# Where attention scores are accumulated: two PSUM banks or six, for the first twenty-one score chunks

## The chip, the core and the metric

The kernel runs on one core of a Trainium2 chip. The core has five engines, each with its own in-order queue of instructions: TensorE (PE in the profile; its weight loads are listed apart, as PEld), VectorE (DVE), ScalarE (ACT), GpSimd (POOL) and SyncE (SP, which here only issues DMAs). They wait for one another by semaphores. Matmuls write into PSUM, which this kernel divides into eight banks of 128 partitions by 512 fp32 values; results leave PSUM through ScalarE and VectorE.

The metric is the device time of one execution in microseconds (us). Before the change the median of three runs is 2384.47 us (2383.08 to 2388.02).

## What is computed

One transformer block on x of shape (2, 2048, 1024), fp32: a pre-norm single-head attention with head size D = 256, then a pre-norm feed-forward part.

```python
x = x + attn(layernorm(x))
x = x + ffn(layernorm(x))

def attn(x):                      # B=2, S=2048, D=256
    q, k, v = split(x @ Wqkv + bqkv)
    p = softmax(q @ k.T / sqrt(D))        # 2048 x 2048 for each of the two sequences
    return (p @ v) @ Wo + bo

def ffn(h):
    rw = sum(top2(h @ gate_w))
    shared = relu(h @ up_w) ** 2 @ down_w
    routed = ((h @ fc1_w @ expert_w) * rw) @ fc2_w
    return layernorm(shared + routed, ln_gamma, ln_beta)
```

## The kernel before

**Precision.** Every large product is made of three fp32r matmuls (`Pass3`, line 117): an operand is split into a high and a low part (`split`, line 140: a cast on ScalarE, a subtraction on VectorE), and high·high, low·high and high·low are added up in one PSUM bank. All these matmuls have line 130 in the profile, so they are told apart by the tile they write.

**Stages.** The 4096 tokens form eight query blocks of 512. First come normalisation and the projections to q, k and v for each block (tiles `pv`, `pq`), in an order written out by hand (`manual_schedule`). Then comes attention (lines 701 to 761), one query block after the other, and then the feed-forward part (from line 1007, again ordered by hand), which takes the rest of the time.

**Attention for query block n.** The 2048 keys of a sequence form 16 chunks of 128.

- `scores(n, k)` (line 545) makes chunk k: two contractions of 128, three matmuls each, so six matmuls of 512 columns into one bank `ps`. ScalarE copies the bank to SBUF (line 557), and VectorE takes the running elementwise maximum from the same bank (line 562; for chunk 0 a second ScalarE copy, line 560).
- `row_max(n)` (line 564), after chunk 15: four small transposes (`pmx`), a reduction on VectorE (line 571), four more transposes (`pmb`).
- `softmax(n, j)` (line 578), for chunks 2j and 2j+1 together: subtract the maximum (line 586, VectorE), exponential (line 587, ScalarE), then a split into the high part (line 142, ScalarE) and the low part (line 143, VectorE) of `p`, and a running sum (lines 593 and 595, VectorE).
- `values(n, k)` (line 597): six matmuls for each chunk, into two banks `po` that stay open over all 16 chunks.
- `finish(n)` and `project(n)` (lines 608 and 629): the row sums (`psum`), the output projection (`pw`, 48 matmuls) and the residual, whose rows come in by DMA from SP and get the bias added by a DMA from POOL.

**Which block runs with which.** `scores(0, 0..15)` stand alone: they come right after the last projection (line 667), with no other large product beside them. Then `start(1)` splits the q of block 1, and `row_max(0)` follows. From there the loop at line 709 pairs `scores(n, k)` with `values(n-1, k-lag)`. For n = 1 the lag is `LAG + 2` = 5, so `scores(1, 0..4)` also come with no `values` beside them. For n > 1 the lag is 3.

**PSUM pools.** `psa` has four banks, `psb` two, `psc` two. Before the change every `ps` bank is one of the two of `psb`. `psa` serves `pv` and `pq` before attention, and `po` (two banks for a whole block) and `pw` within it. `psc` serves the small transposes and the row sums. A bank is handed to its next user when the last reader of the former one is done.

**What sets the order.** The projections and the feed-forward part have their order written out. For attention the Tile framework lays out each engine's queue when the program is built: among instructions that are ready by its own estimate of durations, the one that comes first in the program goes first. On the chip each queue then runs in that fixed order. The POOL queue also carries, within attention, copies and sums of weight matrices for the feed-forward part in DRAM (`sum_step`, line 387).

Of the kernel before, what the change touches and what calls it, by code (L numbers as in the profile page):

```python
# [25 lines left out]
def kernel(  # L26
# [47 lines left out]
    psa = ctx.enter_context(tc.tile_pool(name="psa", bufs=4, space=PSUM))  # L74
    psb = ctx.enter_context(tc.tile_pool(name="psb", bufs=2, space=PSUM))
# [5 lines left out]
    def unit(name, dtype=FR):  # L81
        return up.tile([P, U], dtype, tag="u", name=name)
# [7 lines left out]
    def half(name):  # L90
        return hp.tile([P, W], FP, tag="h", name=name)

    def bank(pool, name):
        return pool.tile([P, W], FP, tag="b", name=name)
# [309 lines left out]
    def hl(t):  # L404

        return t.rearrange("p (s n) -> p s n", s=2)
# [122 lines left out]
    def load_kv(name, src, alloc):  # L529
        t = alloc(name)  # L530
        nc.sync.dma_start(out=f32(t), in_=src)
        return t

    st = {}

    def kv_home(j):
        return ex_unit if j < 2 * BPB - 1 else unit

    def kv_chunk(n, i, k):
        return kv[(n // BPB) * BPB + k // 4][i]  # L540
# [4 lines left out]
    def scores(n, k):  # L545
        s = st[n]
        if k % 4 == 0:
            s["s"].append(unit(f"s{n}_{k // 4}", FP))
        pm = bank(psb, "ps")
        acc = Pass3(pm, NDC)  # L550
        kk, q = hl(kv_chunk(n, 0, k)), hl(s["q"])
        for dc in range(NDC):
            acc.add(
                tuple(kk[:, i, ds(dc * W + (k % 4) * P, P)] for i in range(2)),
                tuple(q[:, i, ts(dc, W)] for i in range(2)),
            )
        nc.scalar.copy(s["s"][k // 4][:, ts(k % 4, W)], pm)  # L557
        if k == 0:
            s["max"] = half(f"max{n}")
            nc.scalar.copy(s["max"], pm)  # L560
        else:
            nc.vector.tensor_tensor(s["max"], pm, s["max"], ALU.max)  # L562
# [34 lines left out]
    def values(n, k):  # L597
        s = st[n]
        if k == 0:
            s["o"] = [Pass3(bank(psa, "po"), NKC) for _ in range(NDC)]  # L600
        v = hl(kv_chunk(n, 1, k))
        for dc in range(NDC):
            s["o"][dc].add(
                tuple(v[:, i, ds((k % 4) * D + dc * P, P)] for i in range(2)),
                tuple(hl(s["p"][k // 2])[:, i, ts(k % 2, W)] for i in range(2)),
            )
# [47 lines left out]
    def a_block(i, norm, xT, x3):  # L654
# [5 lines left out]
        def after(j):  # L660
            if i + 1 == NBLK:
                if j == 0:
                    x3()
                elif j == 2 * NB - 1:
                    start(0, load_row(q_d[0]))
                    for k in range(NKC):
                        scores(0, k)
                    start(1, load_row(q_d[1]))
                    row_max(0)
                return  # L670
            if j == 0:
                x3()
            if j < NB:
                norm.step(j)
            if j == NB - 1:
                norm.step(NB)
                if i + 2 < NBLK:
                    after_next.append(NormBlock(load_block(xf, order[i + 2], nc.gpsimd)))
                nxt.append(new_xT(f"a{i}"))
            elif j > NB:  # L680
                split_tile(norm.x[j - NB - 1], j - NB - 1, nxt[0])
# [22 lines left out]

    g_f = half("g_f")[:, : NCC * NE].rearrange("p (c e) -> p c e", c=NCC)
    nc.gpsimd.dma_start(out=g_f, in_=gate_w.rearrange("(c p) e -> p c e", p=P))
    LAG = 3
    xts = []
    for n in range(1, NBLK + 1):
        if n == NBLK:  # L710
            X = {p: (unit("xh"), unit("xl")) for p in ("p1", "p2")}

        lag = LAG if n > 1 else LAG + 2
        for k in range(NKC + lag):
# [5 lines left out]
            if n < NBLK and k < NKC:  # L720
                scores(n, k)
            if k >= lag:
                values(n - 1, k - lag)
                if n == BPB and (k - LAG) % 4 == 3:
                    j = BPB + (k - LAG) // 4
                    kv[j].append(load_kv(f"v{j}", v_d[j], kv_home(j)))
# [281 lines left out]
    with tc.manual_schedule():  # L1008
        for b in range(NBB):
# [70 lines left out]
            for m, (p, i) in enumerate(UP):  # L1080
# [4 lines left out]
                ps = acc[i].ps  # L1085
# [52 lines left out]
                elif m >= 2 * NK and p != "p7":  # L1138
                    n = {"p4": "p6", "p6": "p5", "p5": "p3", "p3": "p7"}[p]
# [31 lines left out]
            def y_at(r, c, t):  # L1171
                return y[2 * r + t // 2][:, ds((t % 2) * C + c * W, W)]
# [9 lines left out]
            for j, p in enumerate(("p1", "p2", "p6", "p5", "p3", "p7", "p4")):  # L1182
# [12 lines left out]
                for k in range(NK - late):  # L1195
# [4 lines left out]
                    if more:  # L1200
# [3 lines left out]
                        if j >= 5 and k % 2 and k < 2 * NB:  # L1204
                            n = "p1" if j == 5 else "p2"
# [22 lines left out]
                for t in range(NB):  # L1228
                    for s, w in last if late else ():
                        down(t, s, w)  # L1230
                    ps, u, v = accs[t].ps, y_at(1, 0, t), y_at(1, 1, t)
# [72 lines left out]
```

## Time and profile before

| | us |
|---|---|
| median of three runs | 2384.47 |
| profiled execution | 2384.76 |
| its span (first to last instruction) | 2382.9 |
| outside the span | 1.9 |
| PE busy | 2335.8 (98%) |
| PEld busy | 1921.8 (81%) |
| DVE busy | 1461.4 (61%) |
| ACT busy | 1131.4 (47%) |
| POOL busy | 298.1 (13%) |
| first to last start of a `ps` matmul | 309.2 to 719.1 |

A matmul of 512 columns is shown with a duration of about 390 ns, but consecutive ones overlap: they start about 227 ns apart when nothing is in the way. So a PE that is shown busy can still lose time in small pieces, and time lost is better found from the starts than from the busy share. A row of a timeline gives start, duration, engine, line, what is written from what, and in brackets the idle time of the engine before it with the instruction that ended it. A row of the chain gives start, duration and what held it.

### The profile page before, as it was taken

What the parts mean: (1) busy time and instruction counts of PE and PEld (TensorE: products, weight loads), DVE (VectorE), ACT (ScalarE), POOL (GpSimd) and SP (SyncE); (2) the same over time, 40 slices, a digit from 0 to 9 for tenths busy, and PEclk for the clock granted to TensorE, in tenths of its full rate; (3) what the DMA queues carried; (4) which work ended last, traced back from release to release, by engine and by line L of the source; (5) the groups of instructions that cost most, each with busy time, mean ns of one, the idle gap of its engine ahead of it and who ended that gap; (6) DMA issues with size and microseconds to landing.
All of it is one profiled execution on the core that took longest, in us unless ns stands there. A gap on an engine that the chain in (4) does not pass through costs nothing.

```text
span 2382.9 us, 29281 instructions
## 1 busy us (share of the span) xinstructions
PE 2335.8 (98%) x10704; PEld 1921.8 (81%) x10704; DVE 1461.4 (61%) x2168; ACT 1131.4 (47%) x1846; POOL 298.1 (13%) x450
## 2 busy tenths in 40 slices
PE   8999999999998999999999999999999999999998
PEld 7888878888886778788778888878888877888886
DVE  5566459888877466697746467644446563445545
ACT  6555455555444543676552374644145454214224
POOL 3222111012110010011210011210000010000001
PEclk9999999999999999999999999999999999999999
DMA  5977884999996666787997789997557798655695
GB/s 196 318 257 269 278 204 127 298 315 319 290 239 181 219 228 185 228 271 259 336 309 241 237 283 333 319 342 241 193 194 262 264 330 283 208 192 184 202 312 191
DMA packets 225807, 603.99 MB, mean 253 GB/s; under 512 B 18768, under 2 KB 80720, under 8 KB 223616
## 3 DMA queue, kind: packets, MB, share of 16 engines
q1 hardware_dynamic: 152160, 334.02, 41.2%
q0 software_dynamic: 73504, 268.11, 36.8%
q8 instruction: 85, 1.39, 0.2%
q14 instruction: 58, 0.48, 0.1%
HBM read 448.96 MB, written 210.76 MB: 277 GB/s over the span
## 4 chain that ended last, share of the span: by engine, by line
PE 88%; issue 5%; DMA 4%; DVE 1%; ACT 1%; POOL 1%; SPq 0%; POOLq 0%; DVEq 0%; ACTq 0%
PE pu L130 29%; PE pd L130 26%; PE ps L130 7%; PE pq L130 7%; PE po L130 7%; PE pv L130 4%; PE pw L130 3%; DMA w<-wt 1%; PE pg L872 1%; PE pf L130 1%; DMA xt<-xt_d 1%; DMA w<-w_p 1%; PE psum L619 1%; DMA res<-in_L_ffn_ln_beta_dram 0%; DMA ew<-in_L_ffn_expert_w_dram 0%
## 5 line engine op out<-in xcount | busy, mean ns | idle before, releaser
L130 PE MATMUL pd<-w,sp 128*128 128x512 f32 x3336 | 762.5, 390 | 11.0 <-DVE sp L1057 5.6
L130 PEld LDWEIGHTS pd<-w,sp 128*128 128x128 f32 x3336 | 626.5, 188 | 145.8 <-DVE sp L1057 8.4
L130 PE MATMUL pu<-xh,w 128*128 128x512 f32 x2240 | 694.4, 391 | 7.2 <-ACT w L815 5.1
L130 PEld LDWEIGHTS pu<-xh,w 128*128 128x128 f32 x2240 | 419.6, 188 | 99.0 <-ACT w L815 6.1
L130 PE MATMUL pu<-xl,w 128*128 128x512 f32 x1120 | 436.2, 389 | 0.0
L130 PEld LDWEIGHTS pu<-xl,w 128*128 128x128 f32 x1120 | 210.4, 188 | 44.1 <-DVE xl L150 0.4
L1052 ACT CAST sp<-h 128x512 fp32r<-128x512 f32 x238 | 145.9, 618 | 193.1 <-PE pd L130 160.7
L1057 DVE TENSOR_TENSOR sp<-h,sp 128x512 fp32r<-128x512 f32 x238 | 162.4, 687 | 100.9 <-ACT sp L1052 100.6
L815 ACT CAST w<-w 128x512 fp32r<-128x512 f32 x210 | 128.3, 617 | 178.4 <-DMA w<-wt 144.7
L130 PE MATMUL po<-p,v 128*128 128x512 f32 x768 | 197.0, 395 | 2.6 <-ACT p L142 2.4
L823 DVE TENSOR_TENSOR w<-w 128x512 fp32r<-128x512 f32 x210 | 143.1, 686 | 91.3 <-ACT w L815 84.8
L130 PE MATMUL ps<-q,k 128*128 128x512 f32 x768 | 195.9, 393 | 1.8 <-DVE max L562 1.8
L130 PEld LDWEIGHTS ps<-q,k 128*128 128x128 f32 x768 | 142.4, 188 | 36.1 <-DVE max L562 6.8
L130 PEld LDWEIGHTS po<-p,v 128*128 128x128 f32 x768 | 144.1, 190 | 33.6 <-ACT p L142 3.2
L1002 ACT ACTIVATE h<-h 128x1024 f32<-128x1024 f32 x48 | 50.7, 1055 | 208.7 <-DVE h L1110 159.7
L826 POOL DMA_DIRECT2D w_p<-w x140 | 75.1, 537 | 583.1 <-DVE w L823 532.3
L150 DVE TENSOR_TENSOR xl<-xt,xh 128x512 fp32r<-128x512 f32 x104 | 71.6, 688 | 122.8 <-ACT xh L149 120.8
L557 ACT COPY s<-ps 128x512 f32<-128x512 f32 x128 | 74.8, 585 | 148.2 <-PE ps L130 147.7
L213 DVE STREAM_TRANSPOSE xblk<-xrow 128x1024 f32<-128x1024 f32 x60 | 121.1, 2019 | 9.6 <-ACT xrow L283 9.6
L562 DVE TENSOR_TENSOR max<-ps,max 128x512 f32<-128x512 f32 x120 | 82.3, 685 | 44.4 <-ACT s L557 44.1
L130 PE MATMUL pq<-xha,w_h 128*128 128x512 f32 x256 | 99.7, 389 | 0.0
L130 PE MATMUL pq<-xha,w_l 128*128 128x512 f32 x256 | 99.7, 389 | 0.0
(181 smaller groups left out, 3034.3 us busy)
## 6 DMA issues: line engine op xcount, KB each, us to landing
w<-w_p SPq DMA_DIRECT2D x350, 512.0 KB, 4.2
w_p<-w POOLq DMA_DIRECT2D x140, 512.0 KB, 4.8
w<-wt SPq DMA_DIRECT2D x210, 256.0 KB, 3.7
xt_d<-xblk POOLq DMA_DIRECT2D x56, 512.0 KB, 4.6
xt<-xt_d POOLq DMA_DIRECT2D x56, 512.0 KB, 6.6
wt<-in_L_ffn_up_w_dram POOLq DMA_DIRECT2D x9, 2048.0 KB, 25.1
wt<-in_L_ffn_down_w_dram POOLq DMA_DIRECT2D x9, 2048.0 KB, 32.3
xres<-in_L_attn_x_dram SPq DMA_DIRECT2D x32, 512.0 KB, 13.0
```

Source lines behind the costliest of these rows:

```text
L130: nc.tensor.matmul(self.ps, lhsT=a, rhs=b, start=self.i == 0, stop=self.i == self.n - 1, skip_group_check=self.on,)
L150: late_ops.append(lambda: nc.vector.tensor_tensor(lo, t, f32(hi), ALU.subtract))
L213: nc.vector.transpose(b.rearrange("p (q k i) -> p q k i", q=P // SQ, i=SQ), r.rearrange("p (k i q) -> p q k i", k=NCC, i=SQ),)
L557: nc.scalar.copy(s["s"][k // 4][:, ts(k % 4, W)], pm)
L562: nc.vector.tensor_tensor(s["max"], pm, s["max"], ALU.max)
L619: nc.tensor.matmul(pt[:, t : t + 1], lhsT=s["sum"][:, ds(i * W + t * P, P)], rhs=ones, start=i == 0, stop=i == 1,)
L815: nc.scalar.copy(w[:, 0:W], f32(w)[:, W : 2 * W])
L823: nc.vector.tensor_tensor(w[:, W : 2 * W], v[:, W : 2 * W], v[:, 0:W], ALU.subtract)
L826: nc.gpsimd.dma_start(out=kept[key], in_=w.bitcast(FP))
L1002: nc.scalar.activation(o, v, AF.Relu)
L1052: nc.scalar.copy(t[:, 0:W], v)
L1057: add(t[:, W : 2 * W], v, f32(t)[:, 0:W], ALU.subtract)
```

## The change

`scores` takes its bank from `psb` or `psa` in turn for the first twenty-one chunks: of all sixteen of block 0 and of chunks 0 to 4 of block 1, those whose k is a multiple of three still use `psb`, and the others use `psa`. All later chunks use `psb` as before. `LAG` moves up in the file so that `scores` can read it. No instruction is added, removed or resized.

```diff
     st = {}
+    LAG = 3
...
         s = st[n]
         if k % 4 == 0:
             s["s"].append(unit(f"s{n}_{k // 4}", FP))
-        pm = bank(psb, "ps")
+
+        wide = n == 0 or n == 1 and k < LAG + 2
+        pm = bank(psa if wide and k % 3 else psb, "ps")
         acc = Pass3(pm, NDC)
...
-    LAG = 3
     xts = []
```

## The prediction

> **What bounds the kernel.** The page first: PE is busy 98% of the span, and the chain that ended last is 88% PE. So time is gained only where PE itself stands still. The next question is whether it does so where the diff acts. The chain around the start of attention, in order of time:
>
> ```profile
> 287.62 21.79 PE pq L130 x96
> 309.40 21.07 PE ps L130 x84
> ...
> 330.53 1.11 issue
> 331.63 0.70 DVE max L562
> 332.33 0.04 issue
> 332.37 3.04 PE ps L130 x12
> ```
>
> The projections run 96 matmuls in 21.79 us, 0.227 us each, with nothing in between: that is PE's pace. The scores then take 21.07 us for 84, 0.251 each. The timeline of two chunks of block 0 shows why:
>
> ```profile
> 317.62 3.99 PE L130 MATMUL ps<-q,k 128*128 128x512 f32 x15
> 318.04 1.23 PEld L130 LDWEIGHTS ps<-q,k 128*128 128x128 f32 x6 [0.23 <-DVE max L562]
> ...
> 318.29 0.58 ACT L557 COPY s<-ps 128x512 f32<-128x512 f32 x1 [1.02 <-PE ps L130]
> 318.91 0.69 DVE L562 TENSOR_TENSOR max<-ps,max 128x512 f32<-128x512 f32 x1 [0.92 <-ACT s L557]
> 319.65 1.23 PEld L130 LDWEIGHTS ps<-q,k 128*128 128x128 f32 x6 [0.38 <-DVE max L562]
> 319.75 0.59 ACT L557 COPY s<-ps 128x512 f32<-128x512 f32 x1 [0.88 <-PE ps L130]
> ```
>
> The reader is to see that the weight load of each chunk waits for the maximum of the chunk two before it. A bank is emptied by copy and maximum one after the other, from 318.29 to 319.60: 1.3 us, with about 0.1 more on either side. While one bank is emptied, PE fills the other in 6 x 0.227 = 1.36 us. So the bank comes back late each time. The copies at 316.68, 319.75 and 322.81 (each of the same bank) lie 3.07 us apart, 1.53 a chunk: 0.17 us lost on each.
>
> **How much is lost there.** From the starts of matmuls in the timeline: the first score matmul is at 309.24, the first of block 1 at 333.87, the first `po` at 344.03.
>
> - Block 0: 333.87 - 309.24 = 24.63 us, of which 96 x 0.227 = 21.79 is work. Lost: 2.84. Some 14 chunks at 0.17 make 2.4; the rest is one hiccup at 332.37, where the maximum stood behind the split of q (1.23 us, line 143).
> - The five chunks of block 1: 344.03 - 333.87 = 10.16 us, of which 30 x 0.227 = 6.81 and the eight small transposes 0.78 (335.53 to 335.91, 336.94 to 337.34) are work. Lost: 2.57. The largest piece is here:
>
> ```profile
> 342.53 1.23 PEld L130 LDWEIGHTS ps<-q,k 128*128 128x128 f32 x6 [1.80 <-DVE max L562]
> 342.53 1.66 PE L130 MATMUL ps<-q,k 128*128 128x512 f32 x6 [1.36 <-DVE max L562]
> ```
>
> Together 5.41 us is all that more banks could return.
>
> **The Trainium skill, twice.** By "TensorE: Matmul & The Clock Gate", section "Wait — 56ns, not 53.3ns?", warm matmuls of 512 columns start 215.7 ns apart. The row has 227. With the page's figure 126 matmuls would be 1.4 us shorter and the loss 6.8; the unstalled row of this very operation decides, 5.4. And one sentence speaks against the change: the same page, section "HAM oscillation — how this bites in real kernels", says of a tuned kernel that "Adding PSUM double-buffering gave no further gain". By it the sum would be 0. Here two buffers are there already, and the rows show that emptying a bank (1.5 with its gaps) takes longer than filling one (1.36), so I take the row.
>
> **The change, part by part.** Instructions and DMAs stay the same in number and size. What moves:
>
> 1. *Banks of block 0.* With six banks a chunk waits for the maximum of the sixth before it, and five fillings (6.8 us) lie between; ScalarE needs 0.58 and VectorE 0.69 of each 1.36 us, so neither falls behind. `psa` is free: its last users are `pq`, and the last of those is read by line 445 until 310.9; the others have long been read. PE then ends block 0 at 309.24 + 21.79 = 331.03, -2.84. The split of q for block 1 follows the copy of chunk 12 now (328.93, then the cast at 329.41); it should follow it again, some 1.8 us earlier, and be done by 329.9, so block 1 isn't kept waiting.
> 2. *The maximum and what hangs on it.* The last maximum ends at 335.38 now. Then it ends at 331.2 + 0.59 + 0.69 = 332.5, -2.9. Behind it in turn are the transposes, the reduction and the first subtraction (337.62 now), so about 334.7; the load of the exponential's table (1.28), the exponential (1.06), a copy (0.5) and the cast (1.05) give the first high part of `p` at 339.7 (342.70 now).
> 3. *The five chunks of block 1.* PE ends them at 331.03 + 6.81 + 0.78 = 338.6. That is 1.1 us before `p` is there. If nothing stood in between, PE would wait and the gain would be 4.3. But chunk 5 comes ahead of the values in the program, its `psb` bank (chunk 0's) has been read by then, and it takes 1.36, so PE is covered: 5.4. I take the upper end, less 0.3, since the transposes at 335.53 waited 0.29 for the maximum and will again: 5.1.
> 4. *What is late next: VectorE.* In this stretch it is full:
>
> ```profile
> 344.00:382.00 38.00, 38.00 (x175) 31.41 (x173) 36.11 (x39) 23.72 (x32) 0.00 (x0) 1.00 0.21 37
> 382.00:439.00 57.00, 57.00 (x263) 47.14 (x263) 46.72 (x57) 30.06 (x39) 10.15 (x12) 1.00 0.87 233
> ```
>
> (Window, its length, then busy time of PE, PEld, DVE, ACT and POOL.) VectorE is ahead by 2.9, PE by 5.1. The last low part of `p` ends at 377.1 and the last `po` matmul of the block at 381.75; after that part only four matmuls (0.9) must follow, so the block could have ended at 378.0. That leaves 3.7 of slack, and 2.9 + 3.7 = 6.6 is more than 5.1. Inside the stretch a part may be late, but PE has ten score chunks to fill in with. Bounds: gain 2.9 if VectorE decides throughout, 5.4 if never.
> 5. *The rest.* From 344 to 733 PE is busy without a break (57.00 of 57.00 us in the second row, and so in the blocks after it), so a lead is kept. The inputs of the projections come early enough: the bias for the last rows of block 6 lands at 714.91 and they are used from 727.7, 12.8 us of slack. The POOL and SP queues keep their items; their transfers fill the DMA engines (share 1.04 from 400 to 700), but PE waits for none of them. The feed-forward part starts from the end of attention and moves with it.
>
> Sum: the span falls from 2382.9 to 2377.8. The profiled execution (2384.76) is 0.3 above the median, so the same 5.1 is taken from the median: 2384.47 - 5.1 = 2379.4, 0.21% less.
>
> **Rivals.**
>
> - *VectorE decides block 1.* For it: 36.11 of 38.00 busy, and high parts that PE took within tenths of a microsecond of their end. Against it: the slack of 3.7 at the end. Gain 2 to 3.5, about 2381.6.
> - *The banks aren't free when wanted,* `psa` being held by `pq` or kept for `po`, and the change does little: 0 to 1 us, 2384. Against it: the reads of `pq` end by 310.9, and `po` needs two of four.
> - *Another order, slower.* The queues of attention are laid out anew when the program is built, with other bank times. The weak place is where attention ends:
>
> ```profile
> 757.39 9.45 DMA w<-wt
> 766.86 0.62 ACT w L815
> 767.47 0.97 ACT s L587
> 768.46 1.24 DVE sum L595
> 769.70 0.04 issue
> 769.74 3.58 PE psum L619 x16
> ```
>
> A weight transfer of 9.45 us holds a cast on ScalarE, the last exponential stands behind that cast, and PE loses 5.3 and 2.8 us between 761 and 770. Its matmuls after that start 0.43 us apart for a while, 12 x 0.2 = 2.5 us more. If one more such cast or tile load lands ahead of an exponential, it costs about 8 + 2.5 = 10.5. Against the gain: 2384.5 - 5.1 + 10.5 = 2389.9. It decides from a cost of about 10 us on. For it: nothing fixes that order. Against it: the blocks from 2 to 6 repeat 57.3 us apart, so the estimates that lay it out should shift as a whole, and the end with them.
> - *Another order, faster:* the exponential ahead of the cast would return up to 2.8 there: 2376.6.
>
> **Chances.** The sum as told 0.55 (its own range 2377.5 to 2381); VectorE or banks 0.17; slower order 0.20; faster order 0.08. A measurement tells 0.2%, 4.77 us, from nothing: faster is below 2379.7, slower above 2389.2. The predicted 2379.4 stands close to that edge. Of the 0.55 I count 0.42 as faster, since the loss counted by starts is 5.4 and the noise goes either way; with 0.08 that is 0.50. The same: 0.13 + 0.17 = 0.30. Slower 0.20. The range goes from 2375 (the faster order) to 2390 (the slower one at its price).
>
> **What would show it.** Right: score matmuls of block 0 all 0.227 apart, no weight load waiting for line 562 there, first `po` chunk by about 340 with chunk 5 of block 1 ahead of it, the end of block 0's values near 376.7, `po` of the last block some 5 us earlier. Wrong: waits of `po` for lines 142 or 143 between 340 and 375, waits of `ps` for the last reader of `pq`, or a different sequence of ScalarE around the first weight casts. The forecast falls if the lead seen at 345 is gone by 382, or if it is there at 727 and gone by 780.

## The result, and the profile after

| median, us | lowest to highest | runs |
|---|---|---|
| before 2384.79 | 2382.54 to 2389.92 | 6 |
| after 2378.09 | 2377.41 to 2381.34 | 6 |

The medians lie 6.7 us apart. The ratio on record, an estimate from all runs and not exactly the ratio of the two medians (0.9972), is 0.9976 with a 95% interval of 0.9966 to 0.9987: faster by 0.24%, some 6 us. The profiled execution took 2378.47 us with a span of 2376.4, against 2384.76 and 2382.9 before. In the changed file the lines behind the edit are three higher: the copy is 560, the elementwise maximum 565, the subtraction 589, the exponential 590, the row sums' matmul 622. Lines 142 and 143 (the split) stay.

First the chain that ended last, over the start of attention in the kernel after (start, duration, what held it):

```profile
311.06 23.35 PE ps L130 x103
334.40 0.54 PE pmx L572 x4
334.94 0.93 PE ps L130 x4
335.86 0.52 PE pmb L577 x4
...
336.41 1.23 DVE s L589
...
337.71 1.28 ACT L590
...
339.00 1.06 ACT s L590
...
340.57 0.69 DVE max L565
...
342.30 1.23 DVE p L143
...
343.58 0.97 PE po L130 x3
```

103 score matmuls in 23.35 us are 0.227 each, the pace of the projections; before, 84 took 21.07. The chain then leaves PE, for the line from the row maximum through the exponential to the low part of `p`.

The timeline of two chunks of block 0 after, beside which the prediction's fence of the same rows may be laid:

```profile
317.89 0.59 ACT L560 COPY s<-ps 128x512 f32<-128x512 f32 x1 [0.77 <-PE ps L130]
317.93 3.59 PEld L130 LDWEIGHTS ps<-q,k 128*128 128x128 f32 x16
318.51 0.69 DVE L565 TENSOR_TENSOR max<-ps,max 128x512 f32<-128x512 f32 x1 [0.67 <-ACT s L560]
...
319.25 0.59 ACT L560 COPY s<-ps 128x512 f32<-128x512 f32 x1 [0.77 <-PE ps L130]
```

The weight loads have no releaser in brackets any more, and the copies come 1.36 us apart in place of 1.53. Now each reader waits for PE, where PE had waited for the readers.

What the weight loads still wait for from 309 to 385 us (engine, line, what it waited for: us in total, times, longest):

```profile
PEld po L130 <- DVE p L143: 1.0, 1, 1.0
PEld pmx L572 <- PE ps L130: 0.3, 1, 0.3
PEld pmb L577 <- DVE m L574: 0.3, 1, 0.3
```

One wait of a size is left, that of the first `po` chunk for line 143; PE itself waits for nothing else there.

Where the time went, stage by stage, from the starts of matmuls. Each column but the last two counts from the first score matmul: to the first score of block 1 (96 matmuls), to the first `po`, to the row sums of block 0, to those of block 6. Then comes the stretch from there to the last `pw`, the end of attention, and the ratio on record to the kernel before with its interval. From the third row on they are the experiments.

| kernel | block 0 scores | first `po` | sums of block 0 | sums of block 6 | from there to last `pw` | ratio |
|---|---|---|---|---|---|---|
| before | 24.63 | 34.79 | 72.51 | 416.66 | 64.41 | 1 |
| after | 21.76 | 31.03 | 68.21 | 412.29 | 62.55 | 0.9976 (0.9966 to 0.9987) |
| before_again | 24.58 | 34.73 | 72.48 | 416.59 | 62.16 | 0.9998 (0.9990 to 1.0007) |
| after_again | 21.76 | 31.00 | 68.19 | 412.33 | 62.58 | 0.9974 (0.9964 to 0.9983) |
| after_third | 21.76 | 31.01 | 68.27 | 413.53 | 62.00 | 0.9981 (0.9974 to 0.9988) |
| block0_only | 21.76 | 31.91 | 69.65 | 413.78 | 61.97 | 0.9984 (0.9977 to 0.9990) |
| block1_only | 23.89 | 33.85 | 70.02 | 414.25 | 63.27 | 0.9992 (0.9983 to 1.0000) |
| four_banks | 21.76 | 30.57 | 69.75 | 413.99 | 61.48 | 0.9989 (0.9982 to 0.9995) |
| max_from_copy | 21.86 | 31.29 | 69.01 | 413.39 | 62.12 | 0.9979 (0.9969 to 0.9989) |
| low_part_first | 21.76 | 31.02 | 67.82 | 412.15 | 62.73 | 0.9980 (0.9970 to 0.9990) |
| exp_before_cast | 21.76 | 31.03 | 68.23 | 412.36 | 60.58 | 0.9966 (0.9954 to 0.9979) |
| exp_again | 21.76 | 31.05 | 68.20 | 412.38 | 59.81 | 0.9967 (0.9956 to 0.9978) |
| two_banks_exp | 24.60 | 34.75 | 72.51 | 420.56 | 60.22 | 0.9988 (0.9980 to 0.9996) |
| six_banks_low_exp | 21.76 | 31.02 | 67.85 | 412.06 | 59.39 | 0.9971 (0.9961 to 0.9981) |

The first two rows say what the change does: 72.51 - 68.21 = 4.3 us by the end of block 0, of which 2.87 in block 0's scores and 1.43 after them, and 416.66 - 412.29 = 4.37, so still the same 4.3, by the end of block 6.

The spans of these two executions differ by 6.5 us, not 4.3. Before the first score the changed kernel is 1.65 us later (310.89 against 309.24); the end of attention is 1.9 us shorter, and from the last `pw` to the end it is 1.9 us shorter again (1592.5 against 1590.6). These three stages lie outside the edit, and the repeated runs below show how far they move by themselves.

### The profile page after: what moved, and what is told of

Its sections match the earlier page's. It is cut to its first block, busy times and chain, and to the rows that moved or that the text cites. A ratio compares the mean times of both kernels' runs of the same rounds, so it can differ in the third digit from the quotient of the medians.

```text
span 2376.4 us, 29276 instructions
## 1 busy us (share of the span) xinstructions
PE 2331.8 (98%) x10704; PEld 1923.0 (81%) x10704; DVE 1460.5 (61%) x2168; ACT 1132.1 (48%) x1846; POOL 298.1 (13%) x450
## 4 chain that ended last, share of the span: by engine, by line
PE 89%; DMA 5%; issue 4%; ACT 1%; DVE 1%; POOL 0%; SPq 0%; POOLq 0%; DVEq 0%; ACTq 0%
PE pu L130 31%; PE pd L130 25%; PE po L130 7%; PE ps L130 7%; PE pq L130 7%; PE pv L130 4%; PE pw L130 4%; DMA res<-in_L_ffn_ln_beta_dram 2%; PE pg L874 1%; PE pf L130 1%; DMA w<-wt 1%; DMA res<-x 1%; PE psum L622 1%; DMA xt<-xt_d 0%; DMA w_p<-w 0%
```

## The experiments

### The two kernels once more

No edit.

> The kernel before once more, against itself. Expected ratio 1.000. If the stretch ahead of attention, the end of attention and the feed-forward part differ from the first profile by 1 to 2 us each, the surplus of the first comparison over the 4.3 us is what transfers do from one execution to the next; if they agree to 0.3 us, the surplus is the change's.

> The changed kernel once more, for a second profile and a closer interval. Theory (banks alone): from the first score matmul to the first row-sum matmul of block 0 took 72.4 us before and 68.2 after in the first profiles; that 4.2 to 4.3 us should repeat to 0.1, and the time should be 4 to 5 us under the kernel before, about 0.998. Rival (something else moved too): the whole 6.5 us of the first pair of profiles repeats, with the 2 us in the feed-forward part and the 1.7 us at the end of attention at the same places; ratio 0.997.

From the first score matmul to the end of block 6 two profiles of the kernel before agree within 0.1 us. Ahead of that stretch and behind it they do not: the first score matmul starts at 309.2 us in one and at 310.7 in the other, the end of attention took 64.4 and 62.2, the feed-forward part 1592.5 and 1590.9, the whole span 2382.9 and 2380.3. What the changed kernel had lost and gained there in the first pair is of this size. So 4.3 us is what the trace assigns to the edit, and the other 2 are a difference of single executions. Three comparisons of the changed kernel gave 0.9976, 0.9974 and (after_third, 18 runs) 0.9981; each interval holds 0.9982, which is 4.3 us of 2384. That the change has no further effect of a microsecond somewhere is likely by this, not shown.

### Each part alone

Block 0 alone, against the changed kernel:

```diff
-        wide = n == 0 or n == 1 and k < LAG + 2
+        wide = n == 0
```

> Six banks for block 0 alone, two for all of block 1. Theory: block 0 takes 21.8 us from its first matmul to the first of block 1 (24.6 before), 2.8 us off; the five chunks of block 1 still wait for their two banks, though the subtraction that VectorE does for block 0 comes 2.9 us earlier; first score matmul to first row-sum matmul of block 0 about 69.6 (72.4 before, 68.2 with both). Rival (VectorE decides block 1, so only its earlier start counts): the same 68.2 as with both parts.

Block 0 takes 21.76 us as in the whole change, and its values end at 69.65, 2.86 us ahead of before: the lead of block 0's part, undiminished. The wait in block 1 is back. From the waits of its weight loads, and from the timeline of PE:

```profile
PEld ps L130 <- DVE max L565: 2.3, 2, 1.8
```

```profile
339.81 1.43 PE L130 MATMUL ps<-q,k 128*128 128x512 f32 x5 [1.36 <-DVE max L565]
```

It is the 1.80-us wait of the kernel before, at its old size.

The five chunks of block 1 alone:

```diff
-        wide = n == 0 or n == 1 and k < LAG + 2
+        wide = n == 1 and k < LAG + 2
```

> Six banks for the first five chunks of block 1 alone. Theory: block 0 keeps its 24.6 us; block 1 no longer waits, PE reaches the values before the first part of p is there, since p hangs on the last maximum of block 0, which isn't earlier. First score matmul to first row-sum matmul of block 0 between 70.5 and 72.4. Rival (the two parts add up each for itself): 72.4 - 1.5 to 2.6, so 70 to 71, with no wait for p.

The values of block 0 end at 70.02, 2.49 us ahead of before. That is more than I had allowed this part; the rival's expectation is the one that held. Some 0.7 us of it, the 24.63 - 23.89 of the first column, comes from a change of order: the planner put four matmuls of block 1 ahead of the end of block 0's last chunk, and the hiccup of the kernel before at 332.37 is gone. The other waits of block 0 are nearly as they were. Of the 13 in this row 12 lie there, with 3.6 us (before 13 with 4.5, the hiccup's 0.9 among them); the thirteenth, 0.6, belongs to chunk 6 of block 1:

```profile
PEld ps L130 <- DVE max L565: 4.2, 13, 0.6
```

2.86 and 2.49 make 5.35, which is the 5.41 that the prediction had called all that more banks could return. Together they return 4.3. About one microsecond is missing when both are in, and the next section shows where it goes.

### The microsecond that is missing

PE's own timeline in the changed kernel, where the values of block 0 begin:

```profile
340.80 1.29 PE L130 MATMUL ps<-q,k 128*128 128x512 f32 x5
341.93 1.07 PE L130 MATMUL po<-p,v 128*128 128x512 f32 x4
343.58 0.97 PE L130 MATMUL po<-p,v 128*128 128x512 f32 x3 [0.58 <-DVE p L143]
```

And VectorE's at the same time:

```profile
340.57 0.69 DVE L565 TENSOR_TENSOR max<-ps,max 128x512 f32<-128x512 f32 x1
341.18 1.21 DVE L589 TENSOR_TENSOR s<-s,pmb 128x1024 f32<-128x1024 f32 x1
342.30 1.22 DVE L143 TENSOR_TENSOR p<-s,p 128x1024 fp32r<-128x1024 f32 x1
```

Chunk 5 of block 1 does run ahead of the values (the row at 340.80), and the high part of `p`, cast from 340.43 to 341.48, is there in time. But two of the six matmuls of a chunk read the low part. VectorE could start it at 341.5. It stands behind the subtraction of a later pair of chunks, the fourth, and starts at 342.30; that subtraction in turn stood behind the maximum of chunk 2 of block 1 (340.57), whose copy ScalarE made only at 339.96, after the exponential. The four matmuls that need no low part start from 341.93 on and last 4 x 0.227 = 0.91, to 342.84; the next starts at 343.58, 0.74 later. Another 0.11 is lost between that one and its successor, together 0.85 us.

Neither part alone meets this wait. In block0_only the weight loads wait for no part of `p` at all, since the wait for a bank comes first. In block1_only the low part is even later: it starts 0.65 us after the first `po` matmul (343.47 against 342.82), where the changed kernel has 0.37. But there the planner laid five score matmuls behind the first four of the values, and PE loses nothing:

```profile
342.82 1.08 PE L130 MATMUL po<-p,v 128*128 128x512 f32 x4
343.47 1.22 DVE L143 TENSOR_TENSOR p<-s,p 128x1024 fp32r<-128x1024 f32 x1
343.74 1.30 PE L130 MATMUL ps<-q,k 128*128 128x512 f32 x5
```

So PE's own order decides with VectorE's whether this wait is felt.

If the order on VectorE makes the wait, putting the low part ahead of the subtraction should return it:

```diff
-        split(e, hi, lo)
+        nc.scalar.copy(hi, e)
+        s["low"] = nc.vector.tensor_tensor(lo, e, f32(hi), ALU.subtract)
...
-                softmax(0, k // 2)
+                if k == 3:
+                    low_0 = st[0]["low"].ins
+                with tc.issue_after(low_0) if k >= 7 else nullcontext():
+                    softmax(0, k // 2)
```

(`issue_after` makes the planner lay the instructions of the block behind the one named.)

> The changed kernel, with the fourth and later subtractions of block 0 ordered behind the first low part of p on VectorE. In the changed kernel PE loses 0.85 us between 342.6 and 343.6, since that low part stands behind a subtraction and a maximum. Theory: the low part is ready 1.1 us earlier and the wait goes; first score matmul to first row-sum matmul 67.4 (68.2 without). Rival (VectorE is full, so the wait comes back at a later part): 68.2, with a wait of po for line 592 or 142 between 345 and 375.

The 1.0-us wait is gone, but only 0.39 of it is kept at the end of block 0 (67.82 against 68.21) and 0.14 at the end of block 6. The waits of the weight loads from 340 to 372 us say where the rest went:

```profile
PEld po L130 <- DVE p L592: 0.6, 2, 0.4
PEld ps L130 <- DVE max L565: 0.3, 1, 0.3
```

Three smaller waits, all for VectorE, in place of one (line 592 is the low part here). VectorE gives in one place what it takes in another. So the order on VectorE made the one wait; that its return is poor because VectorE has little room in this stretch is what these rows suggest. Against before, 0.9980 can't be told from the changed kernel's ratio.

### How many banks, or how fast one is emptied

Four banks, the second pair from the pool of the small transposes:

```diff
-        pm = bank(psa if wide and k % 3 else psb, "ps")
+        pm = bank(psc if wide and k % 2 else psb, "ps")
```

> The same twenty-one chunks on four banks in place of six: the even ones on the two banks of psb, the odd ones on the two of psc, and psa is left alone. Theory (a bank takes 1.5 us to come back and 1.36 to be filled, so any number over two is enough): block 0 takes 21.8 us from its first matmul to the first of block 1, as with six. In block 1 the two banks of psc are wanted for the transposes of the maximum and one of them is kept through the softmax, so part of that gain goes: first score matmul to first row-sum matmul of block 0 between 68.2 and 69.7. Rival (six are needed): block 0 between 22.5 and 24.6.

In block 0 four do all that six do, 21.76. In block 1 they do not. The weight loads and PE wait here for the high part of `p`, PE's wait and its place being

```profile
PE po L130 <- ACT p L142: 2.2, 1, 2.2
```

```profile
339.58 0.72 PE L130 MATMUL po<-p,v 128*128 128x512 f32 x2 [2.18 <-ACT p L142]
```

The planner laid the values ahead of chunks 4 and 5 in this kernel, so nothing covered the way to `p`. This is the case that step 3 of the prediction called "PE would wait", and with chunk 4 laid behind as well it costs more than the 1.1 us that the prediction had for it. The values of block 0 end at 69.75, 1.54 us later than with six banks. The run doesn't say that four banks are too few as such: another pool was used, which also serves `pmx` and `pmb`, and the order changed with it.

Two banks as before, but each read only once, the maximum being taken from the copy in SBUF:

```diff
-            nc.vector.tensor_tensor(s["max"], pm, s["max"], ALU.max)
+            nc.vector.tensor_tensor(
+                s["max"], s["s"][k // 4][:, ts(k % 4, W)], s["max"], ALU.max
+            )
```

> The kernel before, on two banks, but the running maximum is taken from the copy in SBUF instead of from the bank, for all chunks. A bank is then held for one read of 0.59 us instead of two one after the other (1.3). Theory (the stall is the time to empty a bank): two banks are enough, block 0 takes 21.8 us, and the first stretch to the row sums is near 68.2. Rival (the stall comes from the number of banks or from the order, not from the emptying): 24.6 and 72.5 as before. The time of a maximum may change with its source: 0.69 us is expected again.

A bank is now held by one copy of 0.59 us. Its timeline in block 0:

```profile
316.96 3.36 PEld L130 LDWEIGHTS ps<-q,k 128*128 128x128 f32 x15
317.38 0.59 ACT L557 COPY s<-ps 128x512 f32<-128x512 f32 x1 [0.77 <-PE ps L130]
318.00 0.69 DVE L562 TENSOR_TENSOR max<-s,max 128x512 f32<-128x512 f32 x1 [0.67 <-ACT s L557]
```

Two banks then suffice: 21.86 us for block 0, within 0.1 of six banks. So two banks are not too few as such. What cost time was that one took longer to empty than the other to fill, as step 1 had it, and either cure works: more banks, or one reader less. The maximum costs the same 0.69 us from SBUF. In block 1 one wait remains:

```profile
PE ps L130 <- ACT s L557: 1.2, 1, 1.2
```

The copy is now the only thing that frees a bank, and it stands on ScalarE behind the exponential and its table. The values of block 0 end at 69.01, 0.8 later than with six banks; in the ratio, 0.9979, that can't be seen.

### The exponential behind the weight cast

Both slower and faster orders among the rivals turned on one place: at the end of attention the last exponential of block 7 stands on ScalarE behind a cast of weights that waits for a transfer. The banks did not touch it, which the chain of the changed kernel in its third run shows:

```profile
753.68 9.64 DMA w<-wt
...
763.34 0.62 ACT w L817
...
763.96 0.97 ACT s L590
...
764.95 1.24 DVE sum L598
...
766.23 3.57 PE psum L622 x16
```

The edit orders that cast behind the latest exponential of the program:

```diff
-        nc.scalar.activation(e, e, AF.Exp, scale=SC)
+        last[1] = nc.scalar.activation(e, e, AF.Exp, scale=SC).ins
...
-            nc.scalar.copy(w[:, 0:W], f32(w)[:, W : 2 * W])
+            with tc.issue_after(last[1]):
+                nc.scalar.copy(w[:, 0:W], f32(w)[:, W : 2 * W])
```

> The changed kernel, with the first weight casts on ScalarE ordered behind the last exponential of the last block. Forecast with the rivals: the exponential no longer waits for the weight transfer, the row sums of block 7 come up to 2.8 us earlier. Theory (PE is short of work there for two reasons, weights and row sums): about 2 to 2.8 us less from the row sums of block 6 to those of block 7 (42.0 us in the changed kernel), time 2 us under the changed kernel. Rival (PE has the same matmuls to do and waits for the weights in any case): the row sums move but the last pw matmul does not, within 0.5.

The row sums' wait for VectorE, 2.1 us in each profile of the changed kernel, is gone, and from the row sums of block 6 to the last `pw` it took 60.58 us, where three profiles of the changed kernel have 62.0 to 62.6. Counted from the row sums of block 6, those of block 7 came some 1.4 us earlier, less than the 2 to 2.8 expected. The median of five runs was 2375.18, but they go from 2371.63 to 2379.84 and the profiled one is the slowest. Since they differ by as much as the gain, the kernel was run again beside the changed one:

> Six banks with the weight casts behind the last exponential, once more and beside the changed kernel on the same chip. Theory: 1.9 us under the changed kernel, all of it between the row sums of block 6 and the last pw matmul (60.6 us against 62.6). Rival (the 3 us between the medians of two different calls were chance): the medians within 1 us of each other and the stretch above 62.

> The changed kernel beside it, as the thing to compare with: stretch from the row sums of block 6 to the last pw matmul 62.6 us, first score matmul to first row-sum matmul of block 0 68.2 us, ratio to the kernel before 0.9975 to 0.9982.

2374.88 (seven runs, 2374.14 to 2377.14) against 2378.18 (eighteen, 2377.18 to 2380.64), just without overlap: 3.3 us between the medians, of which the stage itself shows 62.00 - 59.81 = 2.2. This version beats both kernels. The chain of exp_again at the same place:

```profile
751.41 9.47 DMA w<-wt
...
760.96 0.63 ACT w L818
...
761.63 0.79 PE pu L130
762.43 3.20 PE psum L622 x16
```

The exponential and the sum are no longer between the cast and the row sums. The transfer of 9.5 us still is ahead of them, and PE stands for 5 to 6 us.

The granted clock looks like a part of the gain. The windows from 770 to 778 us, of after_third and then of exp_again (window, its length, busy time of PE, PEld, DVE, ACT, POOL, then granted clock, DMA share, GB/s):

```profile
770.00:778.00 8.00, 8.00 (x29) 6.14 (x29) 3.93 (x7) 1.18 (x2) 1.06 (x2) 0.81 0.65 229
```

```profile
770.00:778.00 8.00, 8.00 (x37) 6.30 (x36) 4.38 (x6) 1.18 (x2) 0.00 (x0) 1.00 0.40 162
```

Eight more matmuls in the same 8 us. But this is a shift. The clock is granted at one half from 762.75 to 772.99 us in after_third and from 759.05 to 769.29 in exp_again, 10.24 us in both. The wait of 2.1 us that is gone accounts for the 2.2 of the stage, and for this pair nothing is left for the clock. In the first two profiles of the changed kernel the half clock lasted 13.65 us and the stage took 62.55 and 62.58, so 3.41 us more of it go with some 0.6 us in the stage. All four profiles with this edit have 10.24; of the ten without it seven have 13.65.

Does it need the six banks? The same edit on the kernel before:

> The kernel before, on two banks, with the first weight casts behind the last exponential of the last block. Theory (the two edits act at different places and add up): the stretch to block 0's row sums stays 72.5 us, from the row sums of block 6 to the last pw matmul it is about 60.6 us as with six banks and the same edit (62.2 to 64.4 in the two profiles of the kernel before); ratio 0.999. Rival (the end of attention is shorter only with the lead of the six banks): 62 or more, ratio 1.000.

The end of attention took 60.22 us (before: 64.4 and 62.2), and the ratio is 0.9988. The two gains lie in different places and add up within the noise, some 2 us on each ratio: 0.0012 of 2383 is 2.9 us, with the 4.5 of after_third 7.4, against 7.9 for both in exp_again. In this profile block 6 ends at 420.56, 3.9 us later than before; that is another matter, told under step 5 below.

All together, with the low part of `p` moved too:

> Six banks, the first low part of p ahead of the fourth subtraction, and the weight casts behind the last exponential. Theory: 4.3 + 0.2 + 1.9 = 6.4 us off the kernel before, ratio 0.9973 and below what six banks and the casts give alone by no more than a tenth of a per mille. Rival (the lead is used up at the end of attention, where the weight transfer decides): ratio 0.998.

The first stage is that of low_part_first (67.85 and 67.82), 59.39 is the shortest end of attention by 0.4 us, and the ratio is 0.9971. Moving the low part adds nothing that can be measured.

## Why the prediction was right, step by step

The time, 2379.4, was 1.3 us above the measured 2378.09, and the likeliest case is the one that came. But the parts were not all right, and that the miss is so small is in part luck: the sum was 0.8 too large against the 4.3 us that the edit gives, and the first comparison was some 2 us more favourable than 4.3.

**Step 1, block 0: right.** 24.63 to 21.76, -2.87, where 2.84 was predicted. The Trainium skill's sentence on double-buffering ("TensorE: Matmul & The Clock Gate", "HAM oscillation — how this bites in real kernels"), by which nothing was to be gained, does not carry over to this kernel, and max_from_copy shows why the row decided: a second bank suffices where a bank is emptied faster than the other is filled (one read of 0.59 us), and these were emptied slower (about 1.5 us against 1.36).

**Step 2, the high part of `p`: right.** Foretold 339.7 in the time of before, 30.5 us after the first score; the cast ended at 341.48, 30.6 after it.

**Step 3, the five chunks of block 1: mis-sized.** "so PE is covered: 5.4. I take the upper end, less 0.3" is the step that failed, by 0.8. Chunk 5 covered the wait for the high part, as it said. The chain behind the maximum was followed to that part and no further, and the low part comes later: 0.85 us of waiting, shown above by the rows of PE and VectorE. The 0.3 us taken off for the transposes did not come (0.07 by the starts), so against the 5.4 itself 1.1 is missing; what the 0.85 leaves of it is spread over gaps of a tenth of a microsecond and less. A wait of `po` for line 143 between 340 and 375 was among the prediction's own signs of being wrong, and it came, once. The lower end, 4.3, was named for another reason (PE waits for the high part), which was not what happened with six banks, though it is what four_banks showed, at 2.2 us.

**Step 4, VectorE late next: right in kind, wrong in place.** It was judged by its slack at the end of block 0, 3.7 us, and there it did no harm: the lead of 4.3 at 382 in the time of before was there. But its order, with PE's, decided the 0.85 us at the beginning, and low_part_first shows that it has less room inside the stretch than the slack at its end made it look. The busy share of the whole window did not tell this; the three rows at 341 do. As a rival, "VectorE decides", with 2 to 3.5 us, did not come.

**Step 5, the rest: the lead is kept, but the reason given was too broad.** 4.3 us at block 0, 4.4 at block 6. The slack of 12.8 us was taken at block 6, and only up to its first `pw` matmul; the residual that reads those last rows starts at 737.64, 22.7 after the landing. The tight place is block 4. There the four landings of the bias come 1.9 to 2.4 us ahead of their residuals in the profile before (615.39 to 622.79, read from 617.26 to 625.19), and 0.5 to 0.8 us in the one after (613.99 to 621.62, read from 614.52 to 622.46); blocks 3 and 5 keep 7 us or more in both. "PE waits for none of them" was true of the profile before and is not always true. In two_banks_exp VectorE waited for that bias, and these are its waits from 600 to 640 us and the timeline:

```profile
DVE xres L646 <- DMA xres<-in_L_attn_bo_dram: 2.9, 1, 2.9
```

```profile
628.51 1.22 DVE L595 TENSOR_TENSOR sum<-sum,s 128x1024 f32<-128x1024 f32 x1
629.64 0.74 DVE L646 SCALAR_TENSOR_TENSOR xres<-pw,ri,xres 128x512 f32<-128x512 f32 x1
630.30 0.68 DVE L562 TENSOR_TENSOR max<-ps,max 128x512 f32<-128x512 f32 x1
631.04 2.32 PE L130 MATMUL ps<-q,k 128*128 128x512 f32 x6 [1.98 <-DVE max L562]
```

A late transfer holds the residual, the maximum stands behind the residual, and PE waits for its bank, about 2.1 us. In after_third the same wait cost 1.0. In low_part_first VectorE waits for this bias too (0.9 us), and PE does not. So three of fourteen profiles show it, with two banks and with six, and the kernel before is open to it too. The lead takes from the margin, but the landings move by more: the first of the four comes between 609.1 and 619.6. The runs do not settle whether the lead makes the wait more frequent.

**The rivals.** The banks were free when wanted. The order at the end of attention stayed, so neither the slower case came nor, by itself, the faster one. That the faster one was worth "up to 2.8" is borne out by the edit that forces it: about 2 us in its stage and 3.3 between medians.

## What to carry to other kernels

Ask of a rotating buffer how long one is emptied and how long the others are filled. If emptying is longer, here by two readers in a row, more banks or one reader less cures it; six banks gave block 0 nothing that four had not given (three were not tried). A change of banks is also a change of the order that the planner lays out, so the order is to be read again. When PE is freed, follow the chain to every operand of what comes next, the second half of a split operand too, and look at the order of the engine that makes it, not at its busy share. Gains from two neighbouring waits need not add up: 2.86 and 2.49 made 4.3, since with both gone PE came early enough to meet a third wait.

## What had not been expected of the hardware

After the wait in two_banks_exp (1.98 us idle, 2.1 by the starts) PE did not resume at its pace: the six score matmuls at 631.04 took 2.32 us, eight or nine started 0.43 us apart, and the window after has a granted clock of 0.80:

```profile
632.00:640.00 8.00, 8.00 (x30) 6.46 (x29) 7.11 (x8) 4.18 (x6) 0.00 (x0) 0.80 1.05 286
```

That made the wait of 2.1 us cost 3.7. The clock is granted at one half from 631.78 to 635.19 us, and fully on both sides. Idle times of the same length elsewhere did not do this: after the 2.18 us in four_banks (337.39 to 339.58) the granted clock of the next 4.4 us is 1.00, and after the 1.36 us in block0_only PE ran at 0.227.

What tells the two apart can be worked out from the traces. In all fourteen the granted clock changes only at whole multiples of 3.4133 us, counted from its first change (two_banks_exp: 17.38, then 631.78, which is 180 of them on). Call such a stretch a slot. The 1.98 us of two_banks_exp lie whole in the slot from 628.37 to 631.78, and the half clock follows it. The 2.18 us of four_banks are cut by a slot's end at 337.73, into 0.34 and 1.85. Up to 2360 us all traces together have 9539 slots at full clock. The 29 in which PE stood idle for 1.95 us or more were all followed by half clock; of the eight with 1.75 to 1.90 us three were, and of the rest none. So in these traces a wait costs more once it fills over half of one slot, and where it falls among the slots counts as much as its length. The ends of matmuls are modelled, so the border is known to a tenth of a microsecond at best. The Trainium skill ("TensorE: Matmul & The Clock Gate", "What's actually happening") lets the clock fall after an idle window of about 3.4 us; the length of the slot agrees, but here it need not be idle throughout.
